# Two more of sixteen scan states built by TensorE, and more C products on GpSimd, in the last layer of a four-layer network

## The chip, the core and the metric

The kernel runs on one core of a Trainium2 chip. The metric is the device time of one execution in microseconds, the median of several runs. TensorE (PE) multiplies matrices into PSUM, VectorE (DVE) and ScalarE (ACT) read PSUM and SBUF, GpSimd (POOL) works in SBUF, and SyncE (SP) issues the transfers. Each engine takes its instructions in the order written here, and waits on semaphores for what others must finish first.

## The reference

Four layers run one after the other on x of 8 x 64 x 64 x 64. Only the last, layer 3, is touched. It is a bidirectional Mamba block, once along one image axis and once along the other (two passes s). For each of the 8 images, tokens are normed, projected, passed through a causal convolution and silu, and give per token a step size dt and vectors B and C of 16 states. Then, for every channel and each of the 16 states n, a recurrence runs over the 64 tokens of a row:

```python
def step(h, inp):
    dt_t, B_t, C_t, x_t = inp
    dA = jnp.exp(dt_t[:, :, None] * A)
    h = h * dA + (dt_t * x_t)[:, :, None] * B_t[:, None, :]
    y = jnp.einsum('bdn,bn->bd', h, C_t)
    return (h, y)
```

The output y + D x is multiplied by silu(z) and projected; the forward and the reversed direction (k = 0 and 1) are joined by a linear map, with a residual.

## The kernel before: how layer 3 is tiled and ordered

All is in 32-bit floats. A tile holds 128 partitions by T = 1024 numbers. One **step** is a Step object: pass s, chunk c (half an image, 16 chunks a pass), a quarter g of it, and a direction k. That makes 2 x 16 x 4 x 2 = 256 steps of 16 states, and forward (k = 0) and reversed (k = 1) steps alternate. The text calls the step of k = 0 forward and that of k = 1 reversed; eight steps make a chunk.

The function `stream` (L462) runs one loop over all steps' states, i = 16 * step + n, and emits all engines' instructions by hand (`tc.manual_schedule()`), so the order in the text is the order in each queue. In iteration i:

- `fetch(i + 6)` (L499) issues the load of state i + 6's B and C rows, spread over the partitions, into one of 8 bc buffers.
- `multiply_b(i + 3)` (L523): GpSimd makes hb = du * B.
- `multiply_c(i - 1)` (L559) on GpSimd if state i - 1 is in the list `shared`; the product overwrites the tile h.
- `gather` (L310/L320): TensorE adds a state's product into the accumulator acc with identity matmuls; those of shared states come three iterations late, others two late. At a step's state 0 it first drains the step before (L2190, VectorE) and starts acc with the skip term.
- `scan(i)` (L545): VectorE runs the recurrence as one instruction. A shared state's result goes to a tile h out of 3 buffers; others overwrite their exponent or their hb tile.
- `multiply_c(i)` (L559) on VectorE if the state isn't shared, into one of 3 hc buffers.
- `decay(i + 2)` (L517): ScalarE makes dA = exp(dt * A), into one of the two PSUM tiles of the ring pe.
- `expand(i + 3)` (L2170), only for **direct** states 2, 6, 10 and 14: TensorE makes du * B in the PSUM tile mm (one buffer) by eight 128 x 128 matmuls of du's transpose duT with B on a diagonal. The diagonal lies in DRAM (dg); it is written element by element (L2124) and loaded as a bc tile (L2179). For a direct state the exponent goes to a tile of hb's pool (4 buffers) in SBUF and GpSimd makes no hb.

The next step's preparation (`prepare`, L2089) is cut into pieces by its yields, and `plan` says in which iterations they run, as (ahead of the scan, behind it): n = 2 the conv taps (TensorE, L2099), 3 u (ScalarE, silu), 6 x-projection (L2114), 7 dbl's copy, the transfers of B, C and the four diagonals, the dt matmul (L2128) and dt (softplus, L435), 8 du (GpSimd), 10 z's matmul (L2142), 11 z (silu), 14 transpose (L2160), 15 duT. They all use the one PSUM tile mm, as do expand, the output `finish` (L2203: residual and projection, L2209/L2212, then ScalarE's out, L2228) and the norm's mean (L310) of a chunk to come. `rooms` = (11, 15) are the iterations in which `finish` or the norm may take mm; `finish` of a quarter runs at n = 11 of the next forward step. The task `begin` (L2012) loads and norms the next chunk: raw rows, the root of their mean squares, its inverse broadcast to inv, and xn (GpSimd, L2059).

Of the kernel before, what the change touches and what calls it, by code (L numbers as in the profile page):

```python
# [10 lines left out]
F32 = mybir.dt.float32  # L11
# [7 lines left out]
C = 64  # L19
HW = 64  # L20
L = HW * HW
NS = 16
T = 1024
# [249 lines left out]
class Net:  # L273
# [188 lines left out]
    def stream(self, pools, ahead, steps, behind, rest=None):  # L462
# [18 lines left out]
        nc = self.nc  # L481
        bp, hbp, hcp, hp, pe, pa = pools
        total = len(steps) * NS
        B, CC, hb, dA, hc, acc = {}, {}, {}, {}, {}, {}
# [9 lines left out]
        plan = steps[0].plan  # L494
# [35 lines left out]

        def expand(i):
            if i < total and direct(i):
                while self.held:
                    self.release()
                hb[i] = steps[i // NS].expand(B.pop(i))

        def shared(i):
            return i % NS in steps[i // NS].shared
# [46 lines left out]
        for i in range(total + 2):  # L585
            at, n = divmod(i, NS)
            need(i + ahead[0], "bc")
            need(i + ahead[1], "du")
            fetch_c(i + ahead[2])
            fetch(i + ahead[0])  # L590
            multiply_b(i + ahead[1])
            if 0 < i <= total and shared(i - 1):
                multiply_c(i - 1)


            def begin_next():
                if at + 1 < len(steps) and n == steps[at].start:
                    steps[at + 1].ready()
                    while self.held or self.urgent and not plan:
                        self.advance(behind)  # L600
                    return Task(steps[at + 1].prepare())
                return work

            first = i > NS and n == 2
            if plan:
                before, behind_scan = plan.get(n, (0, 0))
                for _ in range(before if work else 0):
                    work.step()
                work = None if work and work.over else work
                if 2 < i <= total + 2 and shared(i - 3):  # L610
                    gather(i - 3)
                if 1 < i and not first and not shared(i - 2):
                    gather(i - 2)
                self.advance(behind, n in steps[0].rooms)
                if i < total:
                    scan(i)
                work = begin_next()
                for _ in range(behind_scan if work else 0):
                    work.step()
                if first:  # L620
                    gather(i - 2)
                if i < total and not shared(i):
                    multiply_c(i)
                decay(i + 2)
                expand(i + 3)
                continue
            late = i > 1 and not first and steps[0].late and shared(i - 2)
            if i > 1 and not late and not first:
                gather(i - 2)
            work = begin_next()  # L630
            if work is not None and not (self.held and work.said is None) and (calm(i) or not work.calm):
                work.step()
                if work.over:
                    work = None
            room = work is None or work.said is not True and (n < steps[0].early or hasattr(steps[at + 1], "du"))
            self.advance(behind, room, calm(i))
            if late:
                gather(i - 2)
            if i < total:
                scan(i)  # L640
            if first:
                gather(i - 2)
            if i < total:
                if not shared(i):
                    multiply_c(i)
            decay(i + 2)
# [1249 lines left out]
    def layer3(self, src, dst):  # L1896
# [5 lines left out]
        nc, tc = self.nc, self.tc  # L1902
        W, H = 512, 512 // HW
        srcs, dsts = (src, self.hbm["x4"]), (self.hbm["x4"], dst)
        with ExitStack() as ctx:
            pool = lambda n, b, **k: ctx.enter_context(tc.tile_pool(name="l3" + n, bufs=b, **k))
            cp, p1, p2 = pool("c", 1), pool("p1", 1), pool("p2", 2)
            pp = pool("pp", 1, space=PSUM)
# [5 lines left out]
            nc.vector.memset(mean, 1.0 / C)  # L1914
            endless = cp.tile([128, T // HW], F32, name="endless")
            nc.vector.memset(endless, 1e30)

            class Weights:

# [75 lines left out]
            net = self  # L1995
# [3 lines left out]
            inv = cp.tile([128, 4 * H, HW + 6], F32, name="inv")  # L1999
            for t in (*raw, inv):  # L2000
                nc.gpsimd.memset(t, 0.0)
            ends = [slice(3 + r, 3 + r + HW) for r in range(2)]

            fed = (2, 6, 10, 14)
            diags = [hd.tile([len(fed), 128 * 513], F32, name=f"dg{e}") for e in range(2)]
            for e in range(2):
                for n in range(len(fed)):
# [4 lines left out]
            def begin(s, c):  # L2012
# [3 lines left out]
                x = raw[c % 2]  # L2016
                hold = chunks[s, c] = {"x": x}
                from_ = srcs[s][q, rows, part * 4 * W : (part + 1) * 4 * W].rearrange("p (s t) -> p s t", t=HW)
                for r in range(2):
                    nc.sync.dma_start(x[r * C : r * C + C, :, ends[r]], from_)  # L2020
                yield False
                yield False
                rs = p1.tile([128, 16], F32, name="rs")
                for j in range(2):
                    yield CALM_FREE
# [18 lines left out]
                yield False  # L2044
                row = hp.tile([1, 4 * W], F32, name="rs")
                nc.sync.dma_start(row.rearrange("o (p e) -> (o p) e", e=16), rs)
                yield False
                yield False
                for r in range(2):
                    nc.sync.dma_start(  # L2050
                        inv[r * C : r * C + C, :, ends[r]], row.rearrange("o (s t) -> o s t", t=HW).to_broadcast([C, 4 * H, HW])
                    )
                yield False
                yield False
                yield False
                hold["xn"] = p2.tile([128, 4 * H, HW + 6], F32, name="xn")
# [10 lines left out]

            class Step:
                bc_shape, start = [128, 2, W], 2
                direct, rooms = fed, (11, 15)  # L2070
                plan = {2: (0, 1), 3: (1, 0), 6: (0, 1), 7: (2, 0), 8: (1, 0), 10: (0, 1), 11: (1, 0), 14: (0, 1), 15: (1, 0)}
                first = staticmethod(lambda n: 0.0)
                keep = staticmethod(lambda n, h: None)
                shaped = staticmethod(lambda t: t.rearrange("p (j t) -> p j t", j=2))
# [2 lines left out]
                def __init__(self, s, c, g, k):  # L2077
                    self.s, self.c, self.g, self.k, self.rev = s, c, g, k, k == 1
                    self.w = weights[s]
                    self.shared = (1, 2, 5, 6, 9, 10, 13, 14) if k and g % 2 else (1, 2, 5, 6, 9, 10, 14)  # L2080
                    self.diag = diags[k]
                    self.lanes = [(slice(j * W, j * W + W), self.w.A[:, k, j, :]) for j in range(2)]

# [5 lines left out]
                def prepare(self):  # L2089
# [2 lines left out]

                    def tokens(ps):
                        return ps.rearrange("p (s t) -> p s t", t=HW)

                    px = pp.tile([128, T], F32, name="mm")
                    for j in range(2):
# [16 lines left out]
                        nc.tensor.matmul(pd, w.xp[:, k, j, :], u[:, j * W : j * W + W], start=j == 0, stop=j == 1)  # L2114
                    yield True
                    dbl = p2.tile([68, W], F32, name="dbl")
                    nc.scalar.copy(dbl, pd)
                    self.bc = hp.tile([NS, 2, W], F32, name="bc")
                    for m in range(2):
                        nc.sync.dma_start(self.bc[:, m, :], dbl[4 + m * NS : 4 + m * NS + NS])  # L2120
                    for e, n in enumerate(fed):
                        spots = self.diag[e : e + 1].rearrange("o (p x) -> o p x", x=513)[:, :, :W]
                        spots = spots.rearrange("o p (m y) -> o m p y", y=128)[:, :, :, 0]
                        nc.sync.dma_start(spots, dbl[4 + n : 5 + n].rearrange("o (m p) -> o m p", p=128))  # L2124
                    pt = pp.tile([128, T], F32, name="mm")
                    for j in range(2):
                        at = slice(j * C, j * C + 4)
# [8 lines left out]
                    yield  # L2136
                    du = self.du = p2.tile([128, T], F32, name="du")
                    nc.gpsimd.tensor_tensor(du, dt, u, ALU.mult)
                    yield
                    pz = pp.tile([128, T], F32, name="mm")  # L2140
                    for j in range(2):
# [12 lines left out]
                    at = HW - 1 if k else 0  # L2154
                    nc.scalar.copy(dt.rearrange("p (s t) -> p s t", t=HW)[:, :, at], endless)
                    yield
                    px = pp.tile([128, T], F32, name="mm")
                    for m in range(T // 128):
                        at = slice(m * 128, m * 128 + 128)
                        nc.tensor.matmul(px[:, at], du[:, at], net.ident, start=True, stop=True)  # L2160
                    yield True
                    self.duT = p1.tile([128, T], F32, name="duT")
                    nc.scalar.copy(self.duT, px)

                def expand(self, diag):
                    hb = pp.tile([128, T], F32, name="mm")
                    for j in range(2):
                        for m in range(4):
                            at = slice(j * W + m * 128, j * W + m * 128 + 128)
                            nc.tensor.matmul(hb[:, at], self.duT[:, at], diag[:, m * 128 : m * 128 + 128], start=True, stop=True)  # L2170
                    return hb
# [99 lines left out]
```

## Time and profile before

| What | us |
|---|---|
| median of 3 runs | 24387.9 (24381.9 to 24405.93) |
| profiled execution | 24347.66 |
| its span | 24345.9 |
| PE busy | 19665.7 (81%) |
| DVE busy | 21602.2 (89%) |
| ACT busy | 14807.0 (61%) |
| POOL busy | 21248.6 (87%) |

The profile has the busy time of each engine; 40 equal slices of the span; groups of instructions by source line, with count, mean duration, the idle time just before them and what ended it; and a timeline of single instructions. In a timeline the columns are start, duration, engine, line, operation, output and inputs, count, and in brackets the idle time before with its releaser. PEclk is the clock granted to TensorE, 1.00 being full. Layer 3's steps begin near 11,290 us and last to the end.

### The profile page before, as it was taken

Reading aid. Unit: us, or ns where it says so; the run is one execution under the profiler, and the core shown is the slowest. Engines: PE = TensorE matmul, PEld = TensorE weight load, DVE = VectorE, ACT = ScalarE, POOL = GpSimd, SP = SyncE. Lnnn points to the kernel's source line nnn. Section 1 sums busy time; section 2 is a strip of 40 time slices with the busy share of each in tenths; the row PEclk is TensorE's granted clock in tenths of the full one; section 3 lists DMA queues with packets and bytes.
Section 4 is the critical chain, followed back from the end, with each engine's and each line's share of the span. In section 5 each row is a group of like instructions: output and inputs, shape, how many; then the busy total and the mean of one; then the engine's idle time right before and its main releaser. Section 6 shows DMA issues by size and latency. Waiting matters only on the chain. (4 is left out here: it accounts for less than half of the span.)

```text
span 24345.9 us, 270053 instructions
## 1 busy us (share of the span) xinstructions
PE 19665.7 (81%) x91034; PEld 8575.0 (35%) x91034; DVE 21602.2 (89%) x12456; ACT 14807.0 (61%) x19247; POOL 21248.6 (87%) x10196
## 2 busy tenths in 40 slices
PE   7778888888888888887777777777777777777777
PEld 5323333333333223323333333333333333333333
DVE  5599999999998689977999999999999999999999
ACT  5445555555555456614676666666666666666666
POOL 0499999999999579966999999999999999999999
PEclk9889999999999999998999999989999999998999
DMA  3699989989888579923555555555555555555555
GB/s 78 204 327 320 315 312 320 313 312 324 314 311 311 188 266 341 339 61 106 173 174 173 176 173 174 174 170 172 173 174 175 172 176 173 175 172 174 171 173 165
DMA packets 2512624, 5292.03 MB, mean 217 GB/s; under 512 B 1078616, under 2 KB 1084860, under 8 KB 2508928
## 3 DMA queue, kind: packets, MB, share of 16 engines
q1 hardware_dynamic: 2486656, 5211.41, 66.1%
q10 hardware_dynamic: 24576, 63.33, 0.7%
q8 instruction: 718, 11.76, 0.2%
q14 instruction: 674, 5.52, 0.1%
HBM read 5112.98 MB, written 160.31 MB: 217 GB/s over the span
## 5 line engine op out<-in xcount | busy, mean ns | idle before, releaser
L523 POOL TENSOR_TENSOR hb<-du,bc 128x1024 f32<-128x1024 f32 x3584 | 8393.4, 2363 | 682.3 <-DVE h L545 330.2
L545 DVE TENSOR_TENSOR_SCAN dA<-dA,hb 128x1024 f32<-128x1024 f32 x2680 | 6117.1, 2282 | 192.1 <-POOL hb L523 98.8
L523 POOL TENSOR_TENSOR hb<-du,b 128x1024 f32<-128x1024 f32 x2048 | 4834.6, 2391 | 486.4 <-DVE dA L545 214.4
L559 POOL TENSOR_TENSOR h<-h,bc 128x1024 f32<-128x1024 f32 x2016 | 4718.2, 2359 | 64.8 <-DVE h L545 64.7
L517 ACT ACTIVATE dA<-dt,w_A 128x512 f32<-128x512 f32 x6144 | 4188.9, 688 | 617.1 <-DVE hc L559 306.8
L517 ACT ACTIVATE dA<-dt,w_l_A 128x1024 f32<-128x1024 f32 x2560 | 2856.9, 1117 | 1002.3 <-DVE hc L559 762.6
L310 PE MATMUL acc<-hc,ident 128*128 128x512 f32 x7040 | 3380.1, 617 | 91.7 <-DVE img L1347 50.1
L559 DVE TENSOR_TENSOR hc<-dA,bc 128x1024 f32<-128x1024 f32 x2592 | 3174.3, 1225 | 171.8 <-issue 5.3
L2170 PE MATMUL mm<-bc,duT 128*128 128x128 f32 x16384 | 2416.1, 308 | 1043.2 <-ACT dt L435 370.1
L545 DVE TENSOR_TENSOR_SCAN dA<-dA,carry,hb 128x1024 f32<-128x1024 f32 x1320 | 3093.8, 2344 | 105.4 <-POOL hb L523 41.9
L2170 PEld LDWEIGHTS mm<-bc,duT 128*128 128x128 f32 x16384 | 2202.1, 216 | 1878.4 <-ACT dt L435 581.9
L545 DVE TENSOR_TENSOR_SCAN h<-dA,hb 128x1024 f32<-128x1024 f32 x1032 | 2356.6, 2284 | 452.5 <-ACT dA L517 434.3
L545 DVE TENSOR_TENSOR_SCAN h<-hb,mm 128x1024 f32<-128x1024 f32 x1024 | 2321.5, 2267 | 379.7 <-PE mm L2170 207.1
L310 PE MATMUL acc<-h,ident 128*128 128x512 f32 x3200 | 1859.1, 711 | 859.9 <-POOL h L559 833.1
L320 PE MATMUL acc<-hc,ident 64*64 64x512 f32 x17920 | 2219.1, 597 | 0.1
L310 PEld LDWEIGHTS acc<-hc,ident 128*128 128x128 f32 x7040 | 1392.6, 201 | 2084.6 <-issue 1713.0
L320 PE MATMUL acc<-h,ident 64*64 64x512 f32 x14848 | 2004.0, 649 | 113.7 <-POOL h L559 112.9
L559 DVE TENSOR_TENSOR hc<-dA,c 128x1024 f32<-128x1024 f32 x1408 | 1723.8, 1224 | 117.2 <-DMA c<-bc 4.8
L2099 PE MATMUL mm<-xn,taps 128*128 128x512 f32 x2048 | 1124.8, 699 | 581.8 <-DVE h L545 581.6
L559 POOL TENSOR_TENSOR h<-h,c 128x1024 f32<-128x1024 f32 x640 | 1519.3, 2374 | 8.0 <-ACT carry L1330 7.2
L517 ACT ACT_TABLE_LOAD x1159 | 1487.0, 1283 | 20.4
L545 DVE TENSOR_TENSOR_SCAN h<-dA,carry,hb 128x1024 f32<-128x1024 f32 x600 | 1404.6, 2341 | 38.1 <-ACT dA L517 26.2
(331 smaller groups left out, 22983.2 us busy)
## 6 DMA issues: line engine op xcount, KB each, us to landing
bc<-bc SPq DMA_DIRECT2D x3072, 512.0 KB
b<-bc SPq DMA_DIRECT2D x2048, 512.0 KB
c<-bc SPq DMA_DIRECT2D x2048, 512.0 KB
bc<-bc SPq DMA_DIRECT2D x512, 1024.0 KB
bc<-dg SPq DMA_DIRECT2D x1024, 256.0 KB
bc<-bc SPq DMA_DIRECT2D x1024, 256.0 KB
tmp<-rs SPq DMA_DIRECT2D x93, 512.0 KB
raw<-x SPq DMA_DIRECT2D x64, 512.0 KB
```

Source lines behind the costliest of these rows:

```text
L310: self.nc.tensor.matmul(o, lhsT, r, start=start, stop=stop)
L320: self.nc.tensor.matmul(acc[j * C : j * C + C, r * 512 : r * 512 + 512], lhsT(j)[at, at], rhs[at, j * 512 : j * 512 + 512], start=start, s ...
L517: nc.scalar.activation(o[:, cut], s.dt[:, cut], AF.Exp, scale=A[:, n : n + 1])
L523: nc.gpsimd.tensor_tensor(s.shaped(hb[i]), s.shaped(s.du), B.pop(i), ALU.mult)
L545: nc.vector.tensor_tensor_scan(h[:, way], dA[i][:, way], b[:, way], s.first(n), ALU.mult, ALU.add)
L559: engine.tensor_tensor(s.shaped(o), s.shaped(h), CC.pop(i), ALU.mult)
L2099: nc.tensor.matmul(tokens(px[:, j * W : j * W + W]), w.taps[k][:, m, j * 128 : j * 128 + 128], xn[:, :, f : f + HW], start=m == 0, stop=m ...
L2170: nc.tensor.matmul(hb[:, at], self.duT[:, at], diag[:, m * 128 : m * 128 + 128], start=True, stop=True)
```

## The change

1. `fed`, the direct states, become 2, 6, 8, 10, 12 and 14. For 8 and 12 (`lent`) the expansion goes into a PSUM tile of the exponents' ring instead of mm, whose exponent then goes to SBUF. The plan's `expand` doesn't release a held task for these two.
2. `shared`: before, states 1, 2, 5, 6, 9, 10 and 14, and 13 in reversed steps of odd g. After, 13 always, and state 0 in reversed steps: 8 and 9 a step, 8.5 in the mean against 7.25. State 0 is gathered as before in iteration 2, so the loop leaves it out in iteration 3.
3. The diagonal writes, four in one iteration before, are six, put into the plan's iterations 7, 8, 9, 12, 13 and 15.
4. `begin` loads raw and inv in four pieces for each half, one an iteration, in place of two transfers each.
5. A softplus of a 128 x 1 tile ahead of dbl's copy makes ScalarE load the softplus table there.

```diff
         def expand(i):
             if i < total and direct(i):
-                while self.held:
+                while self.held and i % NS not in steps[0].lent:
                     self.release()
-                hb[i] = steps[i // NS].expand(B.pop(i))
+                hb[i] = steps[i // NS].expand(B.pop(i), pe if i % NS in steps[0].lent else None)
...
-                if 2 < i <= total + 2 and shared(i - 3):
+                if 2 < i and shared(i - 3) and (i < NS or n != 3):
                     gather(i - 3)
...
-            fed = (2, 6, 10, 14)
+            fed = (2, 6, 8, 10, 12, 14)
...
-                for r in range(2):
-                    nc.sync.dma_start(x[r * C : r * C + C, :, ends[r]], from_)
-                yield False
-                yield False
+                for g in range(4):
+                    at = slice(g * H, g * H + H)
+                    for r in range(2):
+                        nc.sync.dma_start(x[r * C : r * C + C, at, ends[r]], from_[:, at])
+                        yield False
...
-                for r in range(2):
-                    nc.sync.dma_start(
-                        inv[r * C : r * C + C, :, ends[r]], row.rearrange("o (s t) -> o s t", t=HW).to_broadcast([C, 4 * H, HW])
-                    )
-                yield False
+                for _ in range(4):
+                    yield False
+                row = row.rearrange("o (s t) -> o s t", t=HW)
+                for g in range(4):
+                    at = slice(g * H, g * H + H)
+                    for r in range(2):
+                        nc.sync.dma_start(inv[r * C : r * C + C, at, ends[r]], row[:, at].to_broadcast([C, H, HW]))
+                        yield False
...
-                direct, rooms = fed, (11, 15)
-                plan = {2: (0, 1), 3: (1, 0), 6: (0, 1), 7: (2, 0), 8: (1, 0), 10: (0, 1), 11: (1, 0), 14: (0, 1), 15: (1, 0)}
+                direct, rooms, lent = fed, (11, 15), (8, 12)
+                plan = {2: (0, 1), 3: (1, 0), 6: (0, 1), 7: (2, 0), 8: (1, 0), 9: (1, 0), 10: (0, 1), 11: (1, 0), 12: (1, 0), 13: (1, 0), 14: (0, 1), 15: (1, 0)}
...
-                    self.shared = (1, 2, 5, 6, 9, 10, 13, 14) if k and g % 2 else (1, 2, 5, 6, 9, 10, 14)
+                    self.shared = ((0,) if k else ()) + (1, 2, 5, 6, 9, 10, 13, 14)
...
+                    def place(e):
+                        spots = self.diag[e : e + 1].rearrange("o (p x) -> o p x", x=513)[:, :, :W]
+                        spots = spots.rearrange("o p (m y) -> o m p y", y=128)[:, :, :, 0]
+                        nc.sync.dma_start(spots, dbl[4 + fed[e] : 5 + fed[e]].rearrange("o (m p) -> o m p", p=128))
...
                     dbl = p2.tile([68, W], F32, name="dbl")
+                    net.softplus_act(soft, soft, 0.0)
                     nc.scalar.copy(dbl, pd)
...
-                def expand(self, diag):
-                    hb = pp.tile([128, T], F32, name="mm")
+                def expand(self, diag, pe):
+                    hb = pe.tile([128, T], F32, name="dA") if pe else pp.tile([128, T], F32, name="mm")
```

In the changed program the two new expansions stand in TensorE's queue between the gathers of states 3 and 4 and between those of 7 and 8.

More of the change, by code (lines that the diff above doesn't have):

```diff
@@ L1916, in layer3 @@
             nc.vector.memset(endless, 1e30)
+            soft = cp.tile([128, 1], F32, name="soft")
+            nc.vector.memset(soft, 0.0)
             class Weights:
@@ L2046, in begin @@
                 nc.sync.dma_start(row.rearrange("o (p e) -> (o p) e", e=16), rs)
-                yield False
-                yield False
-                for r in range(2):
-                    nc.sync.dma_start(
-                        inv[r * C : r * C + C, :, ends[r]], row.rearrange("o (s t) -> o s t", t=HW).to_broadcast([C, 4 * H, HW])
-                    )
-                yield False
+                for _ in range(4):
[6 more added lines that the diff above has]
+                        yield False
                 yield False
@@ L2120, in prepare @@
                         nc.sync.dma_start(self.bc[:, m, :], dbl[4 + m * NS : 4 + m * NS + NS])
[L2121 to L2124, printed above, removed]
+                    place(0)
                     pt = pp.tile([128, T], F32, name="mm")
@@ L2138, in prepare @@
                     nc.gpsimd.tensor_tensor(du, dt, u, ALU.mult)
+                    place(1)
+                    yield
+                    place(2)
                     yield
@@ L2156, in prepare @@
                     yield
+                    place(3)
+                    yield
+                    place(4)
+                    yield
                     px = pp.tile([128, T], F32, name="mm")
@@ L2161, in prepare @@
                     yield True
+                    place(5)
                     self.duT = p1.tile([128, T], F32, name="duT")
                     nc.scalar.copy(self.duT, px)
-                def expand(self, diag):
-                    hb = pp.tile([128, T], F32, name="mm")
+                def expand(self, diag, pe):
+                    hb = pe.tile([128, T], F32, name="dA") if pe else pp.tile([128, T], F32, name="mm")
                     for j in range(2):
```

## The prediction

> **What bounds the kernel now.** I read the 40 slices first: layer 3 fills slices 19 to 40. Its first scan lies near 11,290 us and the span ends at 24,345.9, so its 256 steps take about 51 us each. In the stretches from 12,000 to 24,000 us, VectorE is busy 1853 of 2000 us, GpSimd 1873 and TensorE 1562. The groups of that window, shapes kept apart, say who waits (busy time, mean ns of one, idle time before it and what ended it):
>
> ```profile
> L523 POOL TENSOR_TENSOR hb<-du,bc 128x1024 f32<-128x1024 f32 x2826 | 6619.5, 2364 | 591.1 <-DVE h L545 292.5 <-DMA bc<-bc 188.3 <-DVE dA L545 75.1
> ...
> L559 POOL TENSOR_TENSOR h<-h,bc 128x1024 f32<-128x1024 f32 x1707 | 3993.0, 2360 | 58.4 <-DVE h L545 58.3
> ...
> L559 DVE TENSOR_TENSOR hc<-dA,bc 128x1024 f32<-128x1024 f32 x2060 | 2523.1, 1225 | 134.1 <-issue 4.5
> ...
> L545 DVE TENSOR_TENSOR_SCAN h<-hb,mm 128x1024 f32<-128x1024 f32 x942 | 2135.6, 2267 | 356.1 <-PE mm L2170 196.4 <-PE acc L320 112.2 <-POOL hb L523 25.5
> ...
> L545 DVE TENSOR_TENSOR_SCAN h<-dA,hb 128x1024 f32<-128x1024 f32 x765 | 1747.8, 2285 | 394.3 <-ACT dA L517 376.1 <-POOL hb L523 18.1
> ```
>
> GpSimd waits for VectorE, and VectorE for ScalarE and TensorE at a few fixed states; it hardly waits for GpSimd (44 us in all). So VectorE's string of scans sets the pace. Next I read its timeline from 12,000 to 20,000 us and sorted the waits by state. A step without a stall but the one at state 9 takes 48.98 us with nine of VectorE's C products and 47.59 with eight: 1.39 us for each product. The mean before is 8.75 products. Over 8 steps (one chunk) the stalls are about 25.7 us: state 9 8.4 (1.05 in every step), state 5 3.9, state 14 of forward steps 4.3 and of reversed steps 4.7, state 2 2.6, others 1.8. Work without stalls is 47.58 a step; 8 x 47.58 + 25.7 = 406.4.
>
> Where do the stalls come from? TensorE's timeline of one forward step:
>
> ```profile
> 17625.51 3.70 PE L2099 MATMUL mm<-xn,taps 128*128 128x512 f32 x8 [2.01 <-DVE h L545]
> ...
> 17633.00 1.95 PE L320 MATMUL acc<-h,ident 64*64 64x512 f32 x16
> 17634.77 1.90 PE L320 MATMUL acc<-hc,ident 64*64 64x512 f32 x16
> 17637.93 1.93 PE L2114 MATMUL mm<-u,w_xp 128*68 128x512 f32 x4 [1.26 <-DVE h L545]
> 17640.53 1.13 PE L2128 MATMUL mm<-dbl,both 4*128 4x512 f32 x4 [0.67 <-ACT dbl L2117]
> 17643.11 2.05 PE L2170 MATMUL mm<-bc,duT 128*128 128x128 f32 x16 [1.45 <-ACT dt L435]
> ...
> 17650.41 1.14 PE L2142 MATMUL mm<-xn,both 64*128 64x512 f32 x4 [1.66 <-DVE h L545]
> 17652.68 1.97 PE L2209 MATMUL mm<-raw,w_res 64*64 64x512 f32 x2 [1.13 <-ACT z L2151]
> 17654.58 5.56 PE L2212 MATMUL mm<-z,w_end 128*64 128x512 f32 x8
> 17661.36 2.05 PE L2170 MATMUL mm<-bc,duT 128*128 128x128 f32 x16 [1.22 <-ACT out L2228]
> ```
>
> and ScalarE's and VectorE's of the same step:
>
> ```profile
> 17639.90 0.58 ACT L2117 COPY dbl<-mm 68x512 f32<-68x512 f32 x1 [2.75 <-PE mm L2114]
> 17640.50 1.28 ACT L435 ACT_TABLE_LOAD   x1
> 17641.79 1.27 ACT L435 ACTIVATE dt<-mm,w_dtb 128x512 f32<-128x512 f32 x2
> ```
> ```profile
> 17645.89 2.29 DVE L545 TENSOR_TENSOR_SCAN h<-dA,hb 128x1024 f32<-128x1024 f32 x1 [1.05 <-ACT dA L517]
> ...
> 17663.51 2.29 DVE L545 TENSOR_TENSOR_SCAN h<-hb,mm 128x1024 f32<-128x1024 f32 x1 [2.67 <-PE mm L2170]
> ```
>
> The chain scan(6) end 17637.87, L2114, dbl, L2128, dt, exponent of state 9 ends 1.05 us late at scan(9). The chain scan(10), L2142, z, residual L2209 and L2212, out, expand(14) is 2.67 late at scan(14), but only because the residual ran 1.97 + 5.56; in the forward step that begins at 18,032 us it took 1.08 + 3.65 and scan(14) did not wait.
>
> **Part by part, per 8 steps.**
>
> Work moved. GpSimd loses 16 B products and gains 10 C products: -6 x 2.36 = -14 us, and it already waits. VectorE loses 10 C products (six at state 13, four at state 0 of reversed steps): -10 x 1.39 = **-13.9**.
>
> Spread transfers. In one reversed step of a chunk the four diagonal writes hold the DMA queue for 7.29 us, the two inv transfers for 3.15 more, and scan(14) stalls 4.7 us on average. Four pieces in eight issues, one an iteration, and diagonal writes in six places leave such a stall no burst: 4.7 to 0.7, **-4.0**. The two more diagonal writes take 2 x 1.68 us of SP a step; SP waits 32 us a step for buffers and hides them. Twelve extra issues a chunk at 0.4 to 1 us are hidden likewise.
>
> Table load ahead. The dt activation starts at 17641.79, and L2128 ends at 17641.66: with the load gone, dt waits for TensorE instead, since its first half waits for all of L2128. Gain 0.1 us of 1.28. The new 128x1 softplus (nearest row: the 0.21 us copy) and its load fit in ScalarE's 2.75 us idle time.
>
> Expand(8). Built, it stands in TensorE's queue after gather(3) and before gather(4), and waits for scan(5), whose buffer it takes. From L2099 on TensorE has no idle time up to gather(4); then 1.26. Eight matmuls take 1.98 us, so L2114 starts 0.72 later. State 9's stall: 1.05 + 0.72 - 0.09 = 1.68, eight times 13.4 instead of 8.4: **+5.0**. Two xn products that now come together before the C product of state 2 in one step add about **+1.6**.
>
> Expand(12) stands between gathers 7 and 8 and waits for scan(9). It ends some 0.66 us too late for L2142 to start at scan(10)'s end. State 13 no longer has a VectorE product, which takes 1.3 us of cover; and with 13 shared, scan(14) reuses the h tile of state 9, whose gather stands behind expand(14): another 1.0. Slack at full clock was 0.45. So each forward step stalls 0.66 + 1.3 + 1.0 - 0.45, about 2.5 at scan(14); slow clock adds 0.9 (expand(10) runs slow in half of the steps, which now pushes L2142, 0.6; a slow residual in one of ten, 0.3). 4 x 3.4 = 13.6 instead of 4.3: **+9.3**.
>
> State 0 on GpSimd. Before a reversed step scan(1) takes the h tile of state 13, whose gather stands behind expand(2). From scan(14): transpose 2.0, duT 1.1, expand 2.1, gather 1.0, with hand-overs 6.5 us, against 2.2 + 3.45 before scan(1) is due: stall 0.9, four times 3.6. The mean matmul of the next chunk, now in a forward step at iteration 15, puts 3 us ahead of that expand(2) once: +2.6 there, where it cost 2.6 at state 2 before. Sum **+3.6**.
>
> State 5 waits for slow runs of L2099 (5.43 instead of 3.70 us in three of ten); TensorE will idle a little longer before it: **+0.6**. Others **-0.5**.
>
> TensorE gains 16 matmuls a step, 4.1 us, on 40 of 51 busy. The exponents of states 8 and 12 go to SBUF: 4 x 18 ns. GpSimd counted by iteration: after GpSimd's three C products in a row the last ends 1.1 us before its gather would be late. The layer's start has four more 256 KB writes and later raw pieces: 0 to 10 us.
>
> Sum: -13.9 - 4.0 + 5.0 + 1.6 + 9.3 + 3.6 + 0.6 - 0.5 = +1.7 per 8 steps, 32 times: **+54 us**. The profiled execution took 24,347.66 us (span 24,345.9); that makes 24,402. The runs' median, 24,387.9, is 40 us above it; the predicted median is 24,440.
>
> **One rule against the rows.** TensorE's clock was 1.00 up to 18,050 us and 0.50 from 18,052 to 18,054, after gaps of only 0.67 and 1.45 us around L2128. The Trainium skill, "TensorE: Matmul & The Clock Gate", section "Why this matters for your kernels", asks only that no idle gap exceed some 3 us. By it nothing here would run slow: the 0.9 us in scan(14)'s stall and state 5's part would be gone, as in the first rival; I go by the rows.
>
> **Rivals.** A difference within 0.2% (49 us) can't be told from none.
> 1. *Faster: the clock stays up.* Expands 8 and 12 fill TensorE's gaps; the slow part of scan(14)'s stall (3.6 per 8 steps), state 5's 4.5 and half of xn's 1.6 go: -9 from the forecast, 32 x -7.3 = -234, 24,155. For it: the gaps of 1.26 and 1.66 us vanish. Against: those around L2128 and before L2099 stay. Chance 0.30.
> 2. *Slower: GpSimd is late in the reversed step.* If its C product of state 2 ends over 1.1 us later than counted, gather(2), ahead of expand(8) and L2114, holds both; up to the 2.36 us of the inserted product of state 0, less the 0.72 counted: 1.6 x 128 = +205, 24,645. For it: 20 GpSimd operations of 2.36 against 45.2 us of VectorE work. Against: forward stalls let GpSimd catch up. Chance 0.21.
> 3. *As counted on VectorE alone.* If TensorE's new work hides: -17.9 x 32 = -573, 23,815. Against it stands every chain above. Chance 0.06.
> 4. *Forecast*: within 100 us of 24,440, sign open. Chance 0.43, of which 0.05 faster, 0.15 same, 0.23 slower.
>
> Faster 0.30 + 0.06 + 0.05 = 0.41, same 0.15, slower 0.21 + 0.23 = 0.44. The range from 24,100 to 24,700 takes in the first two rivals and a start cost; the forecast's own is 24,340 to 24,540.
>
> **What would show it.** Right: VectorE's C products down to 7.5 a step; scan(9) stalled 1.7 us in every step; scan(14) stalled 2 to 4 us in every forward step, released by acc L320; scan(1) stalled about 0.9 before reversed steps; no DMA among the releasers of scan(14). Wrong, faster: L2170 after dt always near 2.0 us and scan(14) stalled under 1.5. Wrong, slower: L320 waiting for GpSimd's h ahead of expand(8), or scans waiting for hb. If scan(14) is not held by gather(9), my reading of the h tiles fails.

## The result: 1.5% slower, and the profile after

| | before | after |
|---|---|---|
| median, us | 24396.9 (24381.9 to 24411.2, 4 runs) | 24761.3 (24749.3 to 24773.3, 4 runs) |
| ratio to before, 95% interval | 1 | 1.0146 [1.0134, 1.0158] |
| span of the profiled execution | 24345.9 | 24759.5 |
| DVE, POOL, PE busy | 21602.2, 21248.6, 19665.7 | 21239.4, 20880.2, 20627.8 |

The forecast was 24,440 in a range up to 24,700, so the time lies 61 us above the range. The groups of the changed kernel, shapes kept apart, from 12,000 to 24,000 us; the columns are those of the table shown for the kernel before:

```profile
L523 POOL TENSOR_TENSOR hb<-du,bc 128x1024 f32<-128x1024 f32 x2286 | 5381.4, 2361 | 812.2 <-DVE h L545 492.7 <-DVE dA L545 160.8 <-DMA bc<-bc 134.7
...
L559 POOL TENSOR_TENSOR h<-h,bc 128x1024 f32<-128x1024 f32 x1944 | 4550.5, 2358 | 477.8 <-DVE h L545 433.5 <-DMA bc<-dg 31.6 <-DMA bc<-bc 12.4
...
L559 DVE TENSOR_TENSOR hc<-dA,bc 128x1024 f32<-128x1024 f32 x1714 | 2099.1, 1225 | 65.5
...
L545 DVE TENSOR_TENSOR_SCAN h<-hb,mm 128x1024 f32<-128x1024 f32 x914 | 2070.3, 2265 | 526.4 <-PE acc L320 526.3
...
L545 DVE TENSOR_TENSOR_SCAN h<-dA,hb 128x1024 f32<-128x1024 f32 x1029 | 2353.2, 2287 | 954.4 <-ACT dA L517 695.0 <-PE acc L320 222.0 <-POOL hb L523 29.7
```

VectorE's C products fell, from 2060 instructions of this form in the window to 1714, as forecast. But the idle time before the scans rose from 356 to 526 us for `h<-hb,mm` and from 394 to 954 us for `h<-dA,hb`. The releaser of the first changed too: it was mostly `PE mm` (the tile mm), now it is `PE acc` (a gather has to free a tile h). GpSimd waits for VectorE more than before, so it is not what is late.

Sorted by state as in the prediction, from VectorE's timeline between 12,000 and 20,000 us, per 8 steps:

| per 8 steps, us | before | after | measured | forecast |
|---|---|---|---|---|
| work without stalls | 381.9 | 368.3 | -13.6 | -13.9 |
| stall at state 9 | 8.5 | 15.2 | +6.7 | +6.5 (5.0 + 1.6 - 0.1) |
| state 14, forward steps | 4.3 | 14.8 | +10.5 | +9.3 |
| state 14, reversed steps | 4.6 | 4.0 | -0.6 | -4.0 |
| states 1 and 2 together | 2.6 | 8.2 | +5.6 | +3.6 |
| state 5 | 4.4 | 8.6 | +4.2 | +0.6 |
| state 13 | 0.0 | 2.1 | +2.1 | 0 |
| others | 0.9 | 0.0 | -0.9 | -0.5 |
| sum | 407.4 | 421.1 | +13.7 | +1.7 |

(The rows leave 0.3 for rounding and small waits. 13.7 x 32 = 438; the whole layer, from its first direct scan to the end of the span, grew by 389, from 13,046 to 13,435 us. The other 24 us of the spans' difference lie ahead of layer 3, which begins at 11,300 us in the profile of before and between 11,307 and 11,338 in all others. Between the medians the loss is 364 us: the profiled execution of before was 49 us faster than its median.)

One forward step shows three of these stalls. VectorE's timeline:

```profile
17660.66 2.29 DVE L545 TENSOR_TENSOR_SCAN h<-dA,hb 128x1024 f32<-128x1024 f32 x1 [1.54 <-ACT dA L517]
...
17673.93 2.29 DVE L545 TENSOR_TENSOR_SCAN h<-dA,hb 128x1024 f32<-128x1024 f32 x1 [1.89 <-ACT dA L517]
...
17690.66 2.29 DVE L545 TENSOR_TENSOR_SCAN h<-hb,mm 128x1024 f32<-128x1024 f32 x1 [3.15 <-PE acc L320]
```

and TensorE's of the same step:

```profile
17651.13 5.40 PE L2108 MATMUL mm<-xn,taps 128*128 128x512 f32 x8 [3.40 <-DVE h L545]
...
17663.06 2.05 PE L2185 MATMUL dA<-bc,duT 128*128 128x128 f32 x16
17665.04 1.09 PE L320 MATMUL acc<-hc,ident 64*64 64x512 f32 x8
17666.06 1.93 PE L2123 MATMUL mm<-u,w_xp 128*68 128x512 f32 x4
...
17679.28 1.14 PE L2152 MATMUL mm<-xn,both 64*128 64x512 f32 x4
17681.55 1.09 PE L2224 MATMUL mm<-raw,w_res 64*64 64x512 f32 x2 [1.13 <-ACT z L2161]
17682.56 3.65 PE L2227 MATMUL mm<-z,w_end 128*64 128x512 f32 x8
17687.42 2.05 PE L2185 MATMUL mm<-bc,duT 128*128 128x128 f32 x16 [1.21 <-ACT out L2243]
17689.40 1.95 PE L320 MATMUL acc<-h,ident 64*64 64x512 f32 x16
```

Read it from the top. The taps waited 3.40 us for scan(2), which reads mm, and took 5.40 us in place of 3.70: that delays u and the exponent of state 5, and scan(5) stalls 1.54. Expand(8) (`dA<-bc,duT`) stands ahead of the x-projection L2123, and scan(9) stalls 1.89. Expand(14) ends at 17,689.5; gather(9), the first half of the group at 17,689.40, frees the h tile 1 us later, and scan(14) starts at 17,690.66, within that group. It waits for the tile, not for mm.

### The profile page after: what moved, and what is told of

It reads as the page before. It is cut to its first block, busy times and chain, and to the rows that moved or that the text cites. A ratio compares the mean times of both kernels' runs of the same rounds, so it can differ in the third digit from the quotient of the medians.

```text
span 24759.5 us, 288499 instructions
## 1 busy us (share of the span) xinstructions
PE 20627.8 (83%) x99226; PEld 9495.0 (38%) x99226; DVE 21239.4 (86%) x12137; ACT 14814.6 (60%) x19503; POOL 20880.2 (84%) x10004
## 5 line engine op out<-in xcount | busy, mean ns | idle before, releaser
L523 POOL TENSOR_TENSOR hb<-du,bc 128x1024 f32<-128x1024 f32 x3072 | 7222.1, 2361 | 949.7 <-DVE h L545 555.8
L559 POOL TENSOR_TENSOR h<-h,bc 128x1024 f32<-128x1024 f32 x2336 | 5469.8, 2358 | 544.4 <-DVE h L545 494.7
L545 DVE TENSOR_TENSOR_SCAN dA<-dA,hb 128x1024 f32<-128x1024 f32 x1848 | 4214.0, 2280 | 184.3 <-POOL hb L523 102.7
L545 DVE TENSOR_TENSOR_SCAN h<-dA,hb 128x1024 f32<-128x1024 f32 x1352 | 3090.3, 2286 | 1085.4 <-ACT dA L517 800.8
L517 ACT ACTIVATE dA<-dt,w_A 128x512 f32<-128x512 f32 x5120 | 3507.3, 687 | 590.4 <-DVE h L545 320.3
L559 DVE TENSOR_TENSOR hc<-dA,bc 128x1024 f32<-128x1024 f32 x2272 | 2782.2, 1225 | 99.8 <-issue 0.9
L320 PE MATMUL acc<-h,ident 64*64 64x512 f32 x17408 | 2291.1, 641 | 8.3 <-POOL h L559 8.3
L517 ACT ACTIVATE hb<-dt,w_A 128x512 f32<-128x512 f32 x3072 | 2026.5, 707 | 3.9 <-DVE h L545 2.4
L320 PE MATMUL acc<-hc,ident 64*64 64x512 f32 x15360 | 1973.1, 596 | 0.0
L2108 PE MATMUL mm<-xn,taps 128*128 128x512 f32 x2048 | 1233.5, 758 | 758.4 <-DVE h L545 758.4
```

What stands on the lines that cost most here:

```text
L320: self.nc.tensor.matmul(acc[j * C : j * C + C, r * 512 : r * 512 + 512], lhsT(j)[at, at], rhs[at, j * 512 : j * 512 + 512], start=start, s ...
L517: nc.scalar.activation(o[:, cut], s.dt[:, cut], AF.Exp, scale=A[:, n : n + 1])
L523: nc.gpsimd.tensor_tensor(s.shaped(hb[i]), s.shaped(s.du), B.pop(i), ALU.mult)
L545: nc.vector.tensor_tensor_scan(h[:, way], dA[i][:, way], b[:, way], s.first(n), ALU.mult, ALU.add)
L559: engine.tensor_tensor(s.shaped(o), s.shaped(h), CC.pop(i), ALU.mult)
L2108: nc.tensor.matmul(tokens(px[:, j * W : j * W + W]), w.taps[k][:, m, j * 128 : j * 128 + 128], xn[:, :, f : f + HW], start=m == 0, stop=m ...
```

## The experiments

T is the theory: the stalls arise where the table has them, from the order of TensorE's queue and three h tiles. Its rivals in the expectations are G (GpSimd's C products are late) and D (the more and smaller transfers cost the time). Each ratio is to the kernel before, run on the same chip. Stalls are per 8 steps between 12,000 and 20,000 us.

### A fourth h tile (h4), and its control (hc2)

```diff
-            pools = (pool("bc", 8), pool("hb", 4), pool("hc", 3), pool("h", 3), two(pool), pool("pa", 1, space=PSUM))
+            pools = (pool("bc", 8), pool("hb", 4), pool("hc", 2), pool("h", 4), two(pool), pool("pa", 1, space=PSUM))
```

The control has two hc and keeps three h.

> The changed kernel with 4 h tiles in place of 3 (and 2 hc tiles in place of 3, for the room). Theory T (TensorE's queue: scans of shared states wait for an h tile whose gather stands behind an expansion): scan(14) in forward steps waits about 2.7 us in place of 3.7, scan(1) before reversed steps 0 in place of 0.8, and once a chunk about 1.5 in place of 5.6; no scan of a shared state is released by acc L320. Some 11 us less in 8 steps, 24,400 to 24,480. Rival G (GpSimd's nine C products are late) and rival D (element-wise diagonal writes and more small transfers): within 60 us of the changed kernel's 24,761.

> The changed kernel with two buffers for hc in place of three, h kept at three: the control for the run with four h and two hc. Theory (the fourth h buffer alone frees scan(14); the third hc buffer does nothing that counts): 24,730 to 24,830. Rival (fewer C products held back by VectorE, or the new places in the memory, made the gain there): below 24,600.

h4: 24,396 us, 0.9994 [0.9985, 1.0003]. hc2: 24,804 us, 1.0166 [1.0149, 1.0183]. The two runs differ in the fourth h tile alone, and it takes the whole loss back: 4 us under T's range, and far from the 24,761 of G and D. In h4's groups of the same window the scans of direct states again wait mostly for the tile mm:

```profile
L545 DVE TENSOR_TENSOR_SCAN h<-hb,mm 128x1024 f32<-128x1024 f32 x941 | 2131.2, 2265 | 498.3 <-PE mm L2185 320.6 <-PE acc L320 113.9 <-ACT sq L2033 35.4
```

The stall before state 1 is gone (8.2 to 0; 4.7 at state 2, nearly all in the one reversed step of eight that follows the norm's first mean, in its place). T had expected no scan of a shared state to wait for acc L320; at state 2 one does (113.9 us in the line above). State 14's stall falls from 18.8 to 12.8, state 5's from 8.6 to 2.1, state 9's stays at 16.3.

### One part at a time (oldc, c85, spread4, oldbegin, nosoft)

oldc is the changed kernel with the old division of the C products, c85 the kernel before with the new one:

```diff
-                    self.shared = ((0,) if k else ()) + (1, 2, 5, 6, 9, 10, 13, 14)
+                    self.shared = (1, 2, 5, 6, 9, 10, 13, 14) if k and g % 2 else (1, 2, 5, 6, 9, 10, 14)
```

spread4 is the kernel before with `begin` in pieces and the four diagonal writes in the plan's iterations 7, 8, 12 and 13. oldbegin is the changed kernel with `begin` as before, nosoft the changed kernel without this line:

```diff
-                    net.softplus_act(soft, soft, 0.0)
```

> The changed kernel with the old division of C products (7.25 a step on GpSimd), six direct states kept. T: VectorE gets back 10 products of 1.39 us in 8 steps (+13.9), but scan(14) of forward steps has hc(13) ahead of it and no gather(9) to wait for (3.7 to about 1.4), scan(1) has no gather(13) to wait for (-8), state 14 of the one reversed step loses some 2: about 24,650. G: GpSimd has 1.25 products less, VectorE waits less for it: below 24,500. D: 24,761 + 13.9 x 32 = above 25,000, since nothing of the stalls goes.

> The kernel before with the changed division of C products alone (8.5 a step on GpSimd, four direct states). T: GpSimd has 12 + 8.5 + 1 operations of 2.36 us and 0.7 of xn, 51.4 us a step, and becomes the bound with VectorE waiting for hb: 52 to 53 us a step, 24,650 to 24,900; scan(14) of forward steps waits about 1 + 1.3 us more than before. D: no change of transfers, so VectorE's 13.9 us in 8 steps come through: 23,960.

> The kernel before with the spread transfers alone (raw, inv, and its four diagonal writes one an iteration); no other part of the change. T: the reversed step's stall of 4.7 us at scan(14) goes, but the norm's mean matmuls move to iteration 15 of a forward and 11 of a reversed step, where they cost 1 to 3 us: 24,280 to 24,390. D: more and smaller transfers cost time: above 24,450.

> The changed kernel with raw and inv moved in two transfers each and by the old count of iterations; all else as changed. T: the split itself is not what costs, but it sets in which iteration the norm's two mean matmuls take mm; the old count brings back a burst ahead of one scan(14) (4 to 5 us) and takes away one reversed step's 4.0 us: 24,700 to 24,850. D (the small transfers cost): below 24,690.

> The changed kernel without the softplus of one column ahead of dbl's copy, so that the table load stands ahead of dt again. T: the dt activation waits for L2135's matmuls anyway, about 0.1 us is lost a step: 24,760 to 24,800. If the load ahead were worth its 1.28 us in the chain to scan(9): 24,761 + 1.2 x 256 = 25,070. If it were itself a cost (0.3 us and more of ScalarE ahead of dbl): 24,600 to 24,700.

| run | us | ratio | state 1 | state 5 | state 9 | state 14 |
|---|---|---|---|---|---|---|
| oldc | 24,648 | 1.0100 [1.0085, 1.0115] | 0 | 8.3 | 15.1 | 8.7 |
| c85 | 24,752 | 1.0145 [1.0128, 1.0162] | 7.9 | 4.9 | 8.6 | 19.5 |
| spread4 | 24,406 | 0.9997 [0.9987, 1.0006] | 0 | 9.1 | 8.4 | 6.3 |
| oldbegin | 24,782 | 1.0151 [1.0134, 1.0168] | 6.6 | 7.0 | 15.7 | 14.6 |
| nosoft | 24,789 | 1.0152 [1.0137, 1.0167] | 7.1 | 8.8 | 15.9 | 18.8 |

The new division alone costs as much as the whole change: states 1 and 14 stall in c85 without any expand(8) or expand(12). But it isn't the same loss. In c85 GpSimd still makes the products by B of states 8 and 12, so it is busy 7685 of the 8000 us (7002 after), and from 12,000 to 24,000 us the gathers wait 283 us for its products:

```profile
L320 PE MATMUL acc<-h,ident 64*64 64x512 f32 x15560 | 2148.8, 659 | 282.9 <-POOL h L559 280.5
```

The same form waits 4.1 us in the changed kernel, and state 14 stalls in many reversed steps of c85, not in one of eight. So T's time for c85 came true, with GpSimd 96% busy, but VectorE doesn't wait for hb as T said (69 us in that window); GpSimd's lateness shows at the gathers.

Without the division (oldc) the rest costs 1.0%, as T had it: state 9 stays and state 14 is back at 8.7. The parts don't add up: 1.0 and 1.45% against 1.46. At state 14 they nearly do (-0.2 and +10.6 make 10.4, measured +9.9). But c85 also stalls 4.7 us at state 2, 2.0 at state 0, 1.3 at state 10 and 1.3 ahead of the drain, and the changed kernel at none of these.

Spreading the transfers gives nothing: state 14 falls by 2.6 and state 2 by 2.4, but state 5 rises by 4.7. T expected some gain (24,280 to 24,390) and had not counted state 5. In oldbegin the stall of the reversed step at state 14 is gone, as T expected, but no burst comes back there; 3.1 us at state 2 and 2.7 at state 3 take its place, so T's time was right in part by luck. The table load ahead is worth 27 us between medians, 0.1 us a step as forecast, but this isn't clear of noise: the two intervals overlap, and the kernel before differs by 28 us between the two sets of runs.

### The mean left out (nomean)

```diff
-                    ps = pp.tile([128, T], F32, name="mm")
-                    self.mm(ps[:1, :], mean, sq)
-                    yield CALM
-                    nc.scalar.copy(ms, ps[:1, :])
+                    yield False
+                    nc.scalar.copy(ms, sq[:1, :])
```

> The changed kernel with the two matmuls of the norm's mean left out: the mean is taken from one row of the squares instead, so the mean over the channels is not computed, and the one buffer of the tile mm then serves the residual and the taps alone. Theory (the mean's matmul, held back by what GpSimd has still to gather, sits ahead of a chunk's state 1 once and of a reversed step's state 14 once): the 5.6 us ahead of state 1 falls to about 0.8 and the 4.0 us ahead of state 14 of the one reversed step to under 0.7, together some 8 us per 8 steps, 32 times, so 24,440 to 24,520. Rival (these waits are only the place at which an overloaded GpSimd shows; it would show at the next state instead): the 8 us come back at states 5 and 14 of the next steps and the time stays within 24,700 to 24,790.

24,499 us, 1.0041 [1.0026, 1.0056], as T has it. The reversed step's stall at state 14 is gone, and state 1 is at 0.8 in each reversed step; one forward step now waits 0.9 us at state 1 for ScalarE. The two mean matmuls of a chunk cost some 260 us in all. The changed kernel shows why so much, in TensorE's timeline ahead of the scan(1) that stalls 6.39 us:

```profile
17377.24 1.87 PE L310 MATMUL mm<-sq,mean 64*1 64x512 f32 x4 [1.10 <-ACT duT L2178]
17380.20 3.79 PE L2185 MATMUL mm<-bc,duT 128*128 128x128 f32 x16 [1.09 <-ACT sq L2038]
17383.92 3.10 PE L320 MATMUL acc<-h,ident 64*64 64x512 f32 x16
```

The mean puts a matmul, a copy and two hand-overs in front of expand(2), and then expand(2) runs 3.79 us in place of 2.05 and the gathers 3.10 in place of 1.95. The stretches of that time, with the granted clock in the column after the engines:

```profile
17377.20:17379.10 1.90, 1.86 (x4) 0.24 (x4) 1.90 (x2) 1.38 (x2) 1.57 (x1) 1.00 0.75 239
17380.20:17384.00 3.80, 3.80 (x20) 3.58 (x24) 0.00 (x0) 3.23 (x5) 3.80 (x2) 0.50 0.39 139
```

VectorE is at 0.00 in the second: it stands still while the slow expansion and the gather behind it run.

### State 4 in place of state 8 (m4h3 with three h, m4 with four)

```diff
-            fed = (2, 6, 8, 10, 12, 14)
+            fed = (2, 4, 6, 10, 12, 14)
...
-                direct, rooms, lent = fed, (11, 15), (8, 12)
+                direct, rooms, lent = fed, (11, 15), (4, 12)
```

> As h4 (4 h tiles, 2 hc tiles), with state 4 in place of state 8 among the direct states whose expansion lies in the exponents' ring, (4, 12). Its expansion stands in TensorE's queue between gather(15) and the taps matmuls, where TensorE has been idle 2 to 3 us for scan(2), and no longer in the chain from the taps matmuls to dt. Theory T: scan(9) waits 1.0 to 1.2 us in place of 1.9, TensorE's clock stays up for the taps matmuls so that scan(5) hardly waits; about 8 us less in 8 steps than h4's 24,396, that is 24,100 to 24,230. If the place of an expansion in the queue doesn't matter (rivals G and D): within 60 us of 24,396.

> The changed kernel with three h and three hc as it has them, and with state 4 in place of state 8 among the six direct ones, so that expand(8) no longer stands before the x-projection of the next step. Theory (the wait of state 9, 1.9 us in every step, comes from expand(8) ahead of the x-projection; the waits of state 14, 3.5 to 4, come from the three h buffers and stay): state 9 below 1.0, state 14 still 3 or more in the forward steps; the same 324 us as between the two runs with four h, so 24,400 to 24,500. Rival (with three h buffers the time won at state 9 is lost at state 14, because GpSimd sets the pace): 24,650 to 24,790.

m4: 24,072 us, 0.9860 [0.9845, 0.9874], 28 us below T's range. m4h3: 24,258 us, 0.9941 [0.9926, 0.9956], 142 us below T's range. T was right that state 9 falls (15.2 to 7.7) and that state 14 stays with three h tiles (19.2); for m4h3 it overlooked that state 5's 8.6 would go to nothing as well. TensorE's timeline of m4h3 ahead of the taps, and the two stretches:

```profile
17665.27 2.05 PE L2185 MATMUL dA<-bc,duT 128*128 128x128 f32 x16 [0.79 <-DVE h L545]
17667.44 3.77 PE L2108 MATMUL mm<-xn,taps 128*128 128x512 f32 x8
```
```profile
17665.00:17667.40 2.40, 2.05 (x16) 1.86 (x16) 2.40 (x3) 2.14 (x3) 2.40 (x2) 1.00 1.08 229
17667.40:17671.20 3.80, 3.76 (x12) 1.48 (x13) 3.77 (x3) 0.48 (x1) 3.80 (x2) 1.00 0.64 159
```

Expand(4) stands in the gap in which TensorE waited for scan(2), so the taps run at full clock and take 3.77 us; the changed kernel's stretch with the taps that took 5.40, with a clock of 0.69 in the mean, is this:

```profile
17651.00:17656.50 5.50, 5.37 (x12) 2.05 (x12) 5.46 (x5) 0.65 (x1) 5.50 (x4) 0.69 0.46 166
```

Of the taps groups read whole between 12,000 and 20,000 us, those over 5 us are 51 of 155 before, 100 of 147 after, 94 of 154 in spread4, and none of 155 and 156 in m4h3 and m4. State 5's stall goes with them (4.4, 8.6, 9.1, 0 and 2.4 us); m4's 2.4, which no slow taps explain, isn't traced here.

### Five direct states (m5), and four h tiles without the change (b4)

m5 is m4 with this:

```diff
-            fed = (2, 4, 6, 10, 12, 14)
+            fed = (2, 4, 6, 10, 14)
...
-                direct, rooms, lent = fed, (11, 15), (4, 12)
+                direct, rooms, lent = fed, (11, 15), (4,)
...
-                    self.shared = ((0,) if k else ()) + (1, 2, 5, 6, 9, 10, 13, 14)
+                    self.shared = (1, 2, 5, 6, 9, 10, 13, 14)
```

b4 is the kernel before with layer 3's pools as in h4.

> Four h, two hc, and five direct states (2, 4, 6, 10, 14) in place of six: state 12 has its matmul by B on VectorE again as before the change, one tile of the exponentials lent instead of two, and 8 C products on GpSimd in every step. Against the run with (2, 4, 6, 10, 12, 14) it shows what expand(12) is worth. Theory (it costs the wait of state 14 in the forward steps, some 0.65 a step, and saves VectorE one multiply of 1.39 a step): VectorE's product back, 1.39 less 0.7 for half a C product fewer, less about 0.3 a step from the wait, so 24,070 to 24,260. Rival (expand(12) holds up TensorE by more than it saves VectorE): below 24,040.

> The kernel before with four h buffers and two hc buffers in layer 3 in place of three and three, nothing else changed: is the fourth h buffer worth something without the change? Theory (it pays only where states 13 and 0 are shared too, since before the change scan(14) of a forward step waits for the tile mm and not for an h buffer; the two hc buffers cost some 40 us, as they did in the changed kernel): 24,390 to 24,470. Rival (the three h buffers already hold the kernel before, at state 14 of the reversed steps and at state 2): below 24,300, and then the fast versions owe their time to the buffer and not to the change.

m5: 23,973 us, 0.9825 [0.9810, 0.9840], the fastest of all and below T's range. (Its expectation says wrongly that VectorE makes state 12's product by B; it is GpSimd's, and its instructions of that form rise from 3072 to 3328 in the page. VectorE takes back only half a C product a step.) Against m4 the stalls before its scans fall by 9.9 us per 8 steps (27.7 to 17.8), of which 4.3 at state 14 and 2.8 at state 2, and the rest of the time grows by 6.0 (370.5 to 376.5). So the set of m5 is some 100 us faster between medians, on the side of the rival; the two intervals just miss each other (0.9840 and 0.9845). That expand(12) alone costs more than it saves isn't shown, because m5 also gives state 0's product in reversed steps back to VectorE.

b4: 24,808 us, 1.0160 [1.0144, 1.0177]; both theories missed. The stalls before its scans fall from 25.5 to 18.3, but VectorE's C products now wait. The group shown for the kernel before, in b4:

```profile
L559 DVE TENSOR_TENSOR hc<-dA,bc 128x1024 f32<-128x1024 f32 x1994 | 2442.3, 1225 | 746.6 <-PE acc L320 595.5 <-issue 7.1 <-PE mm L2170 0.9
```

746.6 us of idle time against 134.1 with three hc. Per 8 steps, 18.4 of it stand before the product of state 13 alone, which in the changed kernel GpSimd makes. There the third hc is worth at most the 43 us between hc2 and it, and those two intervals overlap. So it depends on the division of the C products which pool is short.

## Why the prediction was wrong

**Where it held.** VectorE's work (-13.6 for -13.9), state 9 (+6.7 for +6.5) and forward state 14 (+10.5 for +9.3, released by acc L320, 3.5 to 3.8 us in every forward step) came as counted; scan(1) stalls 0.8 in three of four reversed steps, forecast 0.9; no DMA is among the releasers of the direct scans. Within state 9 the split was off: it is 1.9 in every step, without the burst put down to two xn. How state 14 divides in forward steps isn't settled: it is 1.1 us in the mean before, 2.7 in c85 without expand(12), 2.7 in h4 without the wait for a tile, and 3.7 in the changed kernel with both.

**The steps that failed**, in all 12.3 us, where the sum was short by 12.0:

1. *"4.7 to 0.7" for reversed state 14* (3.4 us). The burst was there: before, expand(14) of this step waits for its diagonal (first line below). But the change, which spreads the transfers, also puts the norm's second mean at n = 11 of a reversed step, where it holds expand(14) and gather(9) behind it (the other two lines) for 4.0, and the sum has no term for it. In each of the 19 such steps from 12,000 to 20,000 us the mean stands there after the change, and in none before. Leaving the mean out takes the stall to 0, and so does oldbegin, where the mean stands elsewhere. I had followed the h tile only through the residual, which no reversed step has.

```profile
17606.83 3.75 PE L2170 MATMUL mm<-bc,duT 128*128 128x128 f32 x16 [8.24 <-DMA bc<-dg]
```
```profile
17420.59 1.87 PE L310 MATMUL mm<-sq,mean 64*1 64x512 f32 x4 [1.13 <-ACT z L2161]
17424.44 3.78 PE L2185 MATMUL mm<-bc,duT 128*128 128x128 f32 x16 [1.98 <-ACT sq L2038]
```

2. *State 5, "+0.6"* (3.6 us). I had three slow taps in ten and expected "a little" more idle time before them. They became 100 of 147: gaps of 2.9 us and more stood ahead of 69 of 155 groups before and of 125 of 147 after. m4h3, which fills that gap, has no slow taps and no stall at state 5.
3. *"Mean once +2.6"* (2.0 us). The mean also made expand(2) and the gathers run slow (clock 0.50), which is +1.7 and about +0.6.
4. *State 13, no term* (2.1 us). Its exponent and the table load wait for VectorE's product of state 11, since the other PSUM tile is lent to expand(12). It stalls in the runs with expand(12) in the ring (1.9 in oldc, 1.9 in m4, 1.2 in h4) and in none without (before, c85, spread4, m5).
5. *Forward state 14* (1.2 us) was somewhat larger.

**The rivals.** The clock did not stay up where it counts (rival 1): expand(8) and expand(12) fill other gaps than the one before the taps. Rival 2 gave the nearest time, but not by its mechanism: TensorE hardly waits for GpSimd's products ahead of the gathers, by the page of the changed kernel:

```profile
L320 PE MATMUL acc<-h,ident 64*64 64x512 f32 x17408 | 2291.1, 641 | 8.3 <-POOL h L559 8.3
```

**The rule weighed.** The prediction says that by the rule nothing here would run slow. That was wrong by its own kernel, in which gaps of over 3 us stand ahead of 69 of 155 taps groups; I had set the rule aside because of another row, and so did not ask which gaps the change would lift past 3 us. For the changed kernel's taps the Trainium skill, "TensorE: Matmul & The Clock Gate", section "Why this matters for your kernels", was a fair guide: of 147 groups none of the 22 behind a gap under 2.9 us ran slow, and 100 of the 125 behind longer ones did. But the length of a gap doesn't decide. The eight longest gaps of the changed kernel, 3.51 us, were followed by fast taps, and in oldc all 27 gaps of 2.86 to 2.90 us by slow ones. Against the rule stand also the 0.50 after gaps of 1.10 and 1.09 us around the mean, and 2 slow groups of 60 behind gaps under 2 us before the change. What fits better is in the last section.

**Open.** In spread4 103 of 157 taps groups stand behind gaps of over 2.9 us, and why spreading the transfers makes the gaps longer is not shown. Neither is how much of m5's gain over m4 is the lighter TensorE, how much the freed ring tile and how much the division of the C products. The runs don't say either why the layers ahead of layer 3 ended 24 us earlier in the one profile of before.

## What to carry to other kernels

When a product moves from one engine to another, count the buffers on the way of each: here a gather behind an expansion freed the tile, so the fourth tile was worth 1.6% (hc2 to h4), while the same swap of pools in the kernel before cost 1.6%. Put added matmuls where TensorE waits anyway, just ahead of a long matmul that would otherwise run in part at half clock, and not in front of a link of a chain that is already late (state 4 for state 8: 2.0%). Follow a rare piece of work (the mean, two matmul groups in eight steps) through every queue with the tile it holds; it cost 260 us.

## What the runs showed of the hardware

TensorE's granted clock fell to 0.50 after two gaps of only 1.10 and 1.09 us, between which a 1.87 us group of four matmuls with a single weight column ran at 1.00; the sixteen matmuls behind it took 3.79 us in place of 2.05. The same matmuls of the taps took 3.70 us behind short gaps and 5.40 behind one of 3.40.

The clock records of the 14 traces say more than the gaps. From 12,000 to 20,000 us every stretch at 0.50 begins on a grid of 3.41 us that is fixed within a run, and lasts whole periods of it (after the change 259 stretches of one period and 22 of two). A period at full clock in which TensorE was busy under 40% of the time was always followed by one at 0.50 (113 of 113 after, 112 of 112 before), and one busy 80% or more never (0 of 1204 and 0 of 946). If the matmuls of the mean (one column) and of `mm<-dbl,both` (four rows) are not counted as busy, no period busy over half was followed by a slow one in any run. So the share of a period fits these records, and the length of one gap doesn't. That such light matmuls don't hold the clock up is only read from the counts; no run changes them alone.
